# A four-layer convolution and attention sequence on one core: when v's half terms, the later weights, q's terms, the gates and one step of layer 3 are issued

## The chip, the core and the metric

The kernel runs on one core of a Trainium2 chip. The core has a matrix engine (TensorE; in the profile PE for its matmuls and PEld for its weight loads), a vector engine (VectorE, DVE), a scalar engine for activations (ScalarE, ACT), GpSimd (POOL) and SyncE (SP), which here issues nearly all DMAs. Each engine runs its own list of instructions in order, and they wait for each other through semaphores. The metric is the device time of one execution in microseconds (us); the time before is the median of three runs.

## The reference

The input x is eight images of 512 channels by 32 x 32 positions, in f32. Four layers follow one another:

```python
# layer 0: group norm, attention with 8 heads of 64, three inner steps, projection, residual
q, k, v = split(qkv_w @ group_norm(x))
h = softmax(q k^T / 8) v
for _ in range(3): h = h + 0.1 * tanh(inl_w @ h + inl_b)
x = x + proj_w @ h + proj_b
# layer 1: attention over positions, with q and k of 64 channels
x = x + softmax(q1 k1^T) v1
# layer 2: filter up by 2 in both directions, leaky relu, filter down by 2
x = down(leaky(up(x)))
# layer 3: gates from the pooled image mix 8 experts into one set of weights per image
rw = sigmoid(mean(x) @ router_w.T + router_b)
W_i = sum_e rw[e] * w_i[e]
x = relu(bn(W_3 * relu(bn(W_2 * relu(bn(W_1 * x))))) + x)      # 1x1, 3x3, 1x1
```

The gates of an image need layer 2's result of that image only. Layer 3 needs the mixed weights.

## The kernel before

Images are taken one after the other, numbered 0 to 7. For each, `layer0`, `layer1` and, between it and the next image, `between` are called. Layer 3 comes after all of them, for all images; layer 2's result of each image is written to memory (`spilled`, in the profile spill_u) and read back as z.

**Products by half terms.** Every 512 x 512 product with a weight matrix is done by Winograd's form of Strassen's scheme: seven products of quarters instead of eight. The seven are called P1, C11, U2, U3, C22, C21 and C12. Three sums are built up in PSUM (banks A: P1, C11; X: U2, U3, C21; Y: C22, C12); between its terms a bank is read by DVE or ACT. The quarter sums of the data are made on DVE (`quarter_sum`, L515; the sums 0 and 1 serve C22 and U2, the sums 2 and 3 serve U3 and C21), those of the weights lie ready in memory (`stored`) and are loaded as one tile of 1,792 KB by `weight` (L464). `in_turn` (L584) yields after each *half term* (one of the seven for one half u of the output): 14 half terms a product, each four matmuls of 256 columns in v, or two of 512 in q and k. Each matmul stands in the trace as two records. Two orders of the seven exist, `plain` and `alternate` (L593, L594); with `late` the first half of q goes by the plain one and its banks alternate between two PSUM pools.

**The stretch between two images** (`between`, L1346) is written by hand for PE, DVE, ACT and SP: what is called first stands first in each engine's list. It holds layer 1's weighted sum of image b, layer 2 of image b, and q, k and v of image b + 1. Layer 2 of an image goes by two halves e of the channels: `wide` (filter up along the rows, on PE; copies; stores to across_u), `turn` (read back turned), nine `fine_passes` (L1330: `up`, leaky relu, `down`, stores to back_u), `turn_back` (L1282: two reads of 1,024 KB each that need all stores of the half), `narrow` (L1289: two sets of matmuls, the first on the first read), `channels` (L1314: transposes zT, a copy on ACT that sums for the gates, and a spill). `fill` is called twice after each fine pass and issues one half term of k or, when k's 14 are done, of v. So the last v terms are left for the narrow passes:

```python
            for e in range(2):
                two.narrow(e, 0)
                two.narrow(e, 1)
                for _ in range(2):
                    next(value_parts)
                two.channels(e, 0)
                two.channels(e, 1)
                for _ in range(2):
                    next(value_parts)
            all_of(value_parts)
```

The weights rotate through three buffers. The loads of inl (for the inner steps), proj and v1 are issued by SP after q, before v, and at the end.

**Attention of layer 0** (`layer0`, L808) is by hand for PE, DVE and ACT: 64 steps. Step i issues `scores(i)` (four matmuls, exp on ACT, a running sum accs on DVE), then `weighted(i - 2)` (av, four matmuls). The scores' banks come from a pool of two pairs (`ps_sc`), the exps' tiles from the pool `tmp` of six, which other wide temporaries share; half-wide ones have a pool of four. After attention come the three inner steps inl_0 to inl_2, where a planner orders the engines.

**Gates.** `Router` makes them: `sums` (four products and two adds on DVE), `logits` (a matmul with ones into a pair of `ps_sc`, then one DVE operation an image), `gates` (exp on ACT, two DVE operations), `operator` (two DVE operations an image), which makes the matrix that mixes the experts. That for images 0 to 6 stands in image 7's `layer0` after the first two terms of the inner step; that for image 7 in layer 3. `blend_early` and `blend_last` then mix with matmuls (mix, mix_last) into memory.

**The end.** `last_across` (L1405) does layer 1's weighted sum and the wide passes of image 7, `last_rows` its fine passes, `last_columns` its narrow ones, with `lean_images` (L1668) as filling: a chain of steps of layer 3's images 0 and 1 (`first` is the first 1x1 product by halves, in the profile c at L1620; `second` is c2, the 3x3 product, at L1562, and c3 at L1656). The reading of z of image 1 is issued at the end of `last_across`. Images 2 to 7 then run in a loop, in which each round advances the mixing for image 7 by three steps.

Of the kernel before, what the change touches and what calls it, by code (L numbers as in the profile page):

```python
# [17 lines left out]
P = 128  # L18
B, C, H, W = 8, 512, 32, 32
S = H * W  # L20
# [37 lines left out]
def tile_sequence(ctx: ExitStack, tc: tile.TileContext, a: dict, out: bass.AP, shifted: bool):  # L58
# [181 lines left out]
    class Router:  # L240
# [4 lines left out]

        def sums(self):
            n = self.n
            t = tmp(f"parts_{self.name}", S)[:, 0 : n * CC * NE]
            parts = t.rearrange("p (b c e) -> p b c e", b=n, c=CC)
            means = pooled[:, :, self.images].rearrange("p c b -> p b c")  # L250
            for c in range(CC):
                nc.vector.tensor_tensor(
                    parts[:, :, c, :], means[:, :, c].unsqueeze(2).to_broadcast([P, n, NE]),
                    router_w[:, c, :].unsqueeze(1).to_broadcast([P, n, NE]), ALU.mult,
                )
            nc.vector.tensor_add(parts[:, :, 0:2, :], parts[:, :, 0:2, :], parts[:, :, 2:4, :])
            self.parts = parts[:, :, 0, :]
            nc.vector.tensor_add(self.parts, self.parts, parts[:, :, 1, :])
# [14 lines left out]
            nc.vector.reciprocal(at, at)  # L273

        def operator(self, to):
            here = ident.rearrange("p (g e) -> p g e", e=NE)
            for b in range(self.n):
                t = tmp(f"here_{self.name}_{b}", S)[:, 0:P].rearrange("p (g e) -> p g e", e=NE)
                gate = rw[:, self.images, :][:, b, :].unsqueeze(1).to_broadcast([P, NR, NE])
                nc.vector.tensor_tensor(t, here, gate, ALU.mult)  # L280
                nc.vector.tensor_reduce(to[:, b, :], t, AX.X, ALU.add)

    PIECES = WE // HALF
    BLOCK = CC * S // HALF
# [296 lines left out]
        elif u == 0:  # L581
            keep[what] = pair_tmp(f"{name}_{what}")

    def in_turn(name, wt, src, sums_of, made, rows=False, late=False):  # L584

        opened = 0

        terms = {
            "P1": ("A11", src[:, 0:2, 0:HALF]), "C11": ("A12", src[:, 2:4, 0:HALF]),
            "U2": ("S2", 1), "U3": ("S3", 2), "C22": ("S1", 0), "C21": ("-A22", 3),  # L590
            "C12": ("S4", src[:, 2:4, HALF:S]),
        }
        alternate = ("P1", "U2", "C11", "U3", "C22", "C21", "C12")  # L593
        plain = ("P1", "C11", "U2", "U3", "C22", "C21", "C12")  # L594
        opens = {"P1": "A", "U2": "X", "C22": "Y"}
        runs = {"P1": "A", "C11": "A", "U2": "X", "U3": "X", "C21": "X", "C22": "Y", "C12": "Y"}
        for u in range(2):
            banks = {}
            for what in plain if late and u == 0 else alternate:
                part, data = terms[what]  # L600
                part = wt[:, PARTS.index(part)]
                if isinstance(data, int):
                    data = sums_of[data]
                else:
                    data = [data[:, cc] for cc in range(2)]
                if what in opens:
                    pool = (ps_mm, ps_tp)[opened % 2] if late else ps_mm
                    opened += 1
                    banks[opens[what]] = bank(pool, f"{name}_{opens[what]}{u}")
                ps = banks[runs[what]]  # L610
                for s in range(2 if rows else 1):
                    for cc in range(2):
                        if rows:
                            at = (2 * u + s) * P
                            dst, lhs, rhs = ps[:, ts(s, QR)], data[cc][:, at : at + P], part[:, cc]
                        else:
                            dst, lhs, rhs = ps, part[:, cc, ts(u, P)], data[cc]
                        nc.tensor.matmul(  # L618
                            dst, lhs, rhs, start=(what in opens and s == 0 and cc == 0),
                            stop=(cc == 1 and s == rows), skip_group_check=True,  # L620
                        )
                made(what, u, ps)
                yield
# [137 lines left out]
    def queries(b, h, t, w):  # L761
        q = big_tile(f"q_{b}", [P, CC, S])
        made = channels(f"q_{b}", q, qkv_b[:, 0:CC], apart=b > 0)
        if b:
            return q, in_turn(f"q_{b}", w["q"], h, t, made, late=True)
        return q, product(f"q_{b}", w["q"], h, t, made)

    def keys(b, h, t, w):
# [13 lines left out]
    def first_qkv(h, w):  # L782
        made = []
        for mv in channel_stats(0, h):
            pass
        all_of(norm_factors(0, mv, made))
        group_norm(h, *made, nc.vector)
        first_sums(*held["q"], h[:, CC - 1, 0:1])
        t = quarter_sums("h_0", h)
        w["q"] = first_rest(*held["q"])  # L790
        for key in "kv":
            w[key] = weight_sums(key, *held[key], t[3][1][:, 0:1])
        q, parts = queries(0, h, t, w)
        all_of(parts)
        nc.vector.tensor_add(row_bias, row_bias, bias2)
        w["inl"] = weight("inl", 0)
        k, parts = keys(0, h, t, w)
        for _ in range(2):
            next(parts)
        early_exp(0)  # L800
        all_of(parts)
        w["proj"] = weight("proj", 0)
        v, parts = values(0, h, t, w)
        all_of(parts)
        w["v1"] = weight("v1", 0)
        return q, k, v

    def layer0(b, q, k, v, w):  # L808
        hf = big_tile(f"hf_{b}", [P, CC, S])
# [159 lines left out]
        totals = {}  # L969
        engines = mybir.EngineType  # L970
        with tc.manual_schedule(engines={engines.PE, engines.DVE, engines.Activation}):
            for i in range(steps + lag):
                if i < steps:
                    scores(i)
                if i >= lag:
                    weighted(i - lag)
                done = i - lag - SC - 1
                for g in range(1, 2 * PAIRS, 2):
                    closing_pair(g, done - g * SC)
                for g in range(2 * PAIRS, last_g):  # L980
                    closing(g, done - g * SC)
            t_hf = sum_tiles(f"hf_{b}_0")
            name = f"inl_{b}_0"

            def last_total():
                quarter_sum(t_hf, hf, 0, (0, 1))
                for at in range(3):
                    closing(last_g, at)
                quarter_sum(t_hf, hf, 1, (0, 1))
                quarter_sum(t_hf, hf, 0, (2, 3))  # L990
                quarter_sum(t_hf, hf, 1, (2, 3))

            inner = product(
                name, w["inl"], hf, t_hf, inner_step(name, hf), within=last_total
            )
            for _ in range(2):
                next(inner)
            copied(last_g)
# [3 lines left out]
        next(operators, None)  # L1002
        mixing = iter(())
        if b + 1 == B:
            router = Router(0, EARLY)
            router.sums()
            router.logits()
            router.gates()
            router.operator(blend["early"])
            mixing = blend_early()  # L1010
            next(mixing)
        all_of(inner)
# [333 lines left out]
    def between(b, eT, v, inv, y, x, mv, w):  # L1346
# [3 lines left out]
        with tc.manual_schedule(engines=hand):  # L1350
# [19 lines left out]
            q, parts = queries(b + 1, x, t, w)  # L1370
            next(parts)
            two.wide(1, 1, y, (act, act))
            next(parts)
            two.wide(1, 0, y, (act, act))
            two.turn(1)
            for cc in range(2):
                quarter_sum(t, x, cc, (2, 3))
            all_of(parts)
            w["inl"] = weight("inl", b + 1)
            k, parts = keys(b + 1, x, t, w)  # L1380
            v, value_parts = None, None

            def fill():
                nonlocal v, value_parts
                if next(parts, parts) is parts:
                    if v is None:
                        w["proj"] = weight("proj", b + 1)
                        v, value_parts = values(b + 1, x, t, w)
                    next(value_parts)

# [1 line left out]
            for e in range(2):  # L1392
# [3 lines left out]
                    next(value_parts)  # L1396
                two.channels(e, 0)
                two.channels(e, 1)
                for _ in range(2):
                    next(value_parts)  # L1400
            all_of(value_parts)
            w["v1"] = weight("v1", b + 1)
        return q, k, v

    def last_across(b, eT, v, inv, y):  # L1405
        two = Layer2(b)
        act, dve = nc.scalar.copy, nc.vector.tensor_copy
        with tc.manual_schedule(engines=hand):
# [3 lines left out]
            for what, u in weighted_rows(b, eT, v, inv, y):  # L1412
                if (what, u) == ("U3", 1):
                    two.wide(0, 0, y, (act, act))
                elif (what, u) == ("C22", 0):
                    two.wide(0, 1, y, (act, act))
                    two.turn(0)
            two.wide(1, 1, y, (act, dve))
            two.wide(1, 0, y, (act, dve))
            two.turn(1)  # L1420
            zs[1] = load_z(1)
# [255 lines left out]
        zs[b] = load_z(b)  # L1677
        wts[b] = load_weights(b)

    two = last_across(B - 1, *last)  # L1680
    chain = lean_images()
    mixing = blend_last()
    last_rows(two, chain, lambda n: load_image(2) if n == 10 else None)

# [8 lines left out]
    with tc.manual_schedule(engines={engines.PE, engines.DVE, engines.Activation}):  # L1693
# [2 lines left out]
        router = Router(B - 1, 1)  # L1696
        router.sums()
        c1(LEAN + 1, 0)
        router.logits()
        router.gates()  # L1700
        router.operator(blend["last"])
        for b in range(LEAN, B):
            more = b + 1 < B
            if b + 2 < B:
# [5 lines left out]
            h2 = tmp(f"h2_{b}", S)  # L1710
            c2(b, main, 1, True, False)
            nc.scalar.copy(one, main)
            for _ in range(2):
                next(mixing, None)
            c2(b, odd, 3, True, True)
            c2(b, main, 2, False, False)
            nc.scalar.copy(two, main)
# [92 lines left out]
```

## Time and profile before

| | |
|---|---|
| median of three runs | 3608.99 us (3602.99 to 3612.22) |
| the profiled execution's own time | 3608.0 us |
| its span, first to last instruction | 3606.2 us |
| PE busy | 3537.5 us (98%) |
| DVE, ACT busy | 2321.4 us (64%), 1318.1 us (37%) |
| mean granted TensorE clock | 0.994 |
| DMA, mean over the span | 100 GB/s |

A line of the waits tells the waiting engine, what it waited to do and at which line of the kernel, then for whom; then the sum, how often, and the longest. A line of the timeline tells start and duration, the engine, line and operation, what it writes and reads, its shape and count; in brackets the engine's idle time before it and who ended it. Busy time of overlapping matmuls is counted once.

### The profile page before, as it was taken

How to read it: one execution, taken by the hardware profiler on the slowest of the kernel's cores; microseconds unless marked ns; L12 is line 12 of the kernel's file. 1: busy time of each engine (PE TensorE's matmuls, PEld its weight loads, DVE VectorE, ACT ScalarE, POOL GpSimd, SP SyncE). 2: the span in 40 equal slices, each digit the busy share in tenths (PEclk: the TensorE clock that was granted, in tenths of full speed). 3: DMA queues.
4: the chain of work that ended last, by engine and by line, in shares of the span. 5: the costliest groups of instructions: out<-in, count | busy, mean ns of one | idle time of the engine just before them, and what ended most of it. 6: DMA issues, size and time to landing. Idle time of an engine off the chain costs nothing.

```text
span 3606.2 us, 47891 instructions
## 1 busy us (share of the span) xinstructions
PE 3537.5 (98%) x19445; PEld 1758.9 (49%) x19445; DVE 2321.4 (64%) x3130; ACT 1318.1 (37%) x1740; POOL 102.1 (3%) x140
## 2 busy tenths in 40 slices
PE   8999999999999999999999999999999999999998
PEld 4336543474435643465434743356434744347333
DVE  4787558755676557774677657775577656755544
ACT  0632345223442236323452235422362234432443
POOL 4100000000000000000000000000000000010000
PEclk9999999999999999999999999999999999999999
DMA  5102441115211350024411251023411152232783
GB/s 202 39 30 85 128 144 42 44 58 188 74 36 64 114 178 16 27 85 142 136 36 64 78 182 45 30 85 120 152 42 44 53 182 84 100 109 73 250 322 117
DMA packets 149032, 360.86 MB, mean 100 GB/s; under 512 B 17792, under 2 KB 92560, under 8 KB 142144
## 3 DMA queue, kind: packets, MB, share of 16 engines
q1 hardware_dynamic: 144336, 338.56, 28.1%
q0 software_dynamic: 4320, 18.87, 1.5%
q8 instruction: 155, 2.54, 0.3%
q14 instruction: 77, 0.63, 0.1%
q10 hardware_dynamic: 144, 0.26, 0.0%
HBM read 226.55 MB, written 118.49 MB: 96 GB/s over the span
## 4 chain that ended last, share of the span: by engine, by line
PE 93%; DMA 4%; DVE 2%; ACT 1%; SPq 0%; issue 0%; DVEq 0%; ACTq 0%
PE scores L838 12%; PE av L883 12%; PE inl_X L559 7%; PE av_X L1192 5%; PE inl_Y L559 5%; PE inl_A L559 4%; PE av_A L1192 3%; PE av_Y L1192 3%; PE v_X L559 3%; PE c L1562 2%; PE proj_X L559 2%; PE k_X L618 2%; PE up L1251 2%; PE v_Y L559 2%; PE dn L1269 2%; PE v_A L559 2%
## 5 line engine op out<-in xcount | busy, mean ns | idle before, releaser
L857 ACT ACTIVATE e<-scores 128x1024 f32<-128x1024 f32 x504 | 516.4, 1025 | 420.0 <-PE scores L838 369.2
L838 PE MATMUL scores<-q,k 64*64 64x512 f32 x4096 | 530.7, 591 | 0.0
L883 PE MATMUL av<-e,v 64*64 64x512 f32 x4096 | 528.7, 589 | 0.0
L867 DVE TENSOR_TENSOR accs<-accs,e 128x1024 f32<-128x1024 f32 x240 | 294.2, 1226 | 50.9 <-ACT e L857 47.2
L883 PEld LDWEIGHTS av<-e,v 64*64 64x64 f32 x4096 | 156.6, 133 | 282.8 <-issue 274.6
L838 PEld LDWEIGHTS scores<-q,k 64*64 64x64 f32 x4096 | 152.8, 133 | 289.9 <-issue 256.2
L559 PE MATMUL inl_X<-T_hf,w_inl 128*128 128x512 f32 x576 | 262.0, 593 | 0.4 <-DVE inl_U L714 0.3
L1258 DVE TENSOR_TENSOR fine<-up,fine 128x1024 f32<-128x1024 f32 x128 | 150.7, 1219 | 112.0 <-ACT fine L1257 108.8
L1257 ACT ACTIVATE fine<-up 128x1024 f32<-128x1024 f32 x128 | 124.0, 1020 | 159.8 <-PE up L1251 159.8
L559 PE MATMUL inl_A<-hf,w_inl 128*128 128x512 f32 x384 | 176.2, 601 | 3.7 <-DVE hf L700 3.7
L559 PEld LDWEIGHTS inl_X<-T_hf,w_inl 128*128 128x128 f32 x576 | 108.5, 190 | 138.8 <-issue 111.0
L703 ACT ACTIVATE inl_U<-inl_U,inl_b 128x512 f32<-128x512 f32 x96 | 67.0, 719 | 291.1 <-DVE inl_U L718 291.1
L904 DVE RECIPROCAL inv<-av 128x256 f32<-128x256 f32 x80 | 138.9, 1745 | 0.0
L714 DVE TENSOR_TENSOR inl_U<-inl_X,inl_P 128x512 f32<-128x512 f32 x96 | 61.8, 685 | 109.2 <-PE inl_X L559 109.2
L865 DVE TENSOR_TENSOR accs<-e,e 128x1024 f32<-128x1024 f32 x48 | 59.7, 1244 | 100.1 <-ACT e L857 81.1
L1192 PE MATMUL av_A<-v,eT 128*128 128x256 f32 x512 | 122.6, 383 | 0.0
L559 PEld LDWEIGHTS inl_A<-hf,w_inl 128*128 128x128 f32 x384 | 71.9, 191 | 101.4 <-issue 85.7
L1192 PE MATMUL av_X<-v,eT 128*128 128x256 f32 x512 | 114.0, 381 | 0.0
L1229 ACT COPY wide<-wide 128x1024 f32<-128x1024 f32 x62 | 59.8, 1015 | 135.6 <-PE wide L1221 135.6
L1081 ACT ACTIVATE eT<-scores 128x512 f32<-128x512 f32 x128 | 66.1, 603 | 115.5 <-PE scores L386 115.5
L1192 PEld LDWEIGHTS av_X<-v,eT 128*128 128x128 f32 x512 | 96.6, 190 | 19.3 <-DVE av_U L1166 6.5
L867 DVE TENSOR_TENSOR acc<-acc,e 128x1024 f32<-128x1024 f32 x80 | 96.8, 1210 | 8.4 <-ACT e L857 7.6
(398 smaller groups left out, 5551.5 us busy)
## 6 DMA issues: line engine op xcount, KB each, us to landing
x<-in_x_dram SPq DMA_DIRECT2D x64, 512.0 KB, 6.0
across_u<-wide SPq DMA_DIRECT2D x128, 256.0 KB, 3.7
turned<-across_u SPq DMA_DIRECT2D x64, 512.0 KB, 5.9
back_u<-sent SPq DMA_DIRECT2D x256, 128.0 KB, 2.3
back<-back_u SPq DMA_DIRECT2D x32, 1024.0 KB, 7.1
w_v<-stored_u_v SPq DMA_DIRECT2D x14, 1792.0 KB, 7.3
out_dram<-z SPq DMA_DIRECT2D x31, 512.0 KB, 3.0
spill_u<-z SPq DMA_DIRECT2D x28, 512.0 KB, 5.8
```

The lines of the kernel that those rows point to most:

```text
L559: nc.tensor.matmul(dst, lhs, rhs, start=(opens and s == 0 and cc == 0), stop=(cc == 1 and s == rows), skip_group_check=True,)
L618: nc.tensor.matmul(dst, lhs, rhs, start=(what in opens and s == 0 and cc == 0), stop=(cc == 1 and s == rows), skip_group_check=True,)
L838: nc.tensor.matmul(ps[r][rows[c]], k[rows[r], oc, jc * P + c * HD : jc * P + c * HD + HD], q[rows[r], oc, ts(sh, HALF)], start=True, stop= ...
L857: nc.scalar.activation(e, pair, AF.Exp, scale=HD ** -0.5)
L867: nc.vector.tensor_add(accs[g], accs[g], e)
L883: nc.tensor.matmul(avs[g][r][rows[c]], v[rows[r], jc, ts(2 * oc + c, HD)], e[rows[r], ts(c, HALF)], start=(jc == 0), stop=(jc == SC - 1),)
L904: nc.vector.reciprocal(copies[g][:, at], totals[g][:, at])
L1192: nc.tensor.matmul(ps[:, ts(s, QR)], left[:, j, at : at + P], right[:, j, :], start=(what in ("P1", "U2", "C22") and s == 0 and j == 0), s ...
L1251: nc.tensor.matmul(pairs[g // 2][HD * s : HD * s + HD, ts(g % 2, HALF)], up_v[part, :], self.turned[e][part, first : first + 2, :], start= ...
L1257: nc.scalar.mul(t, ps, 0.2)
L1258: nc.vector.tensor_max(t, ps, t)
L1269: nc.tensor.matmul(banks[s][W * g : W * g + W, :], dn_v[part, :], fine[g // 2][part, ts(g % 2, HALF)], start=True, stop=True,)
```

## The change

Five things are issued at another place; no arithmetic changes.

1. In `between`, after the first pair of `channels` four half terms of v are issued instead of two, so that none is left after the last pair of terms.
2. In `between`, the loads of inl and proj are issued at the end, ahead of that of v1.
3. q's first half goes in the order `alternate`, as its second half, k and v do; the quarter sums 2 and 3 are called one place earlier. `late` is called `two_pools` now and only chooses the pools.
4. The gates of images 0 to 6 are made in image 7's attention: from step 3 on, each step issues a piece of `early_router`: the sums at step 3, logits and gates at step 4, then one image's operator a step. Their temporaries come from the half-wide pool.
5. `last_across` takes the first step of `lean_images` between its last two wide passes (the weights' transform and half of image 0's first product), so the chain runs one step ahead of where it was; and in layer 3's loop the gates of image 7 are made inside the first round, in the place of its first two mixing steps.

```diff
+        def operators(self, to):
             here = ident.rearrange("p (g e) -> p g e", e=NE)
             for b in range(self.n):
-                t = tmp(f"here_{self.name}_{b}", S)[:, 0:P].rearrange("p (g e) -> p g e", e=NE)
+                t = tmp(f"here_{self.name}_{b}")[:, 0:P].rearrange("p (g e) -> p g e", e=NE)
...
                 nc.vector.tensor_reduce(to[:, b, :], t, AX.X, ALU.add)
+                yield
...
-            for what in plain if late and u == 0 else alternate:
+            for what in alternate:
...
+    def early_router():
+        router = Router(0, EARLY)
+        router.sums()
+        yield
+        router.logits()
+        router.gates()
+        yield
+        yield from router.operators(blend["early"])
...
+            router = iter(early_router() if b + 1 == B else ())
             for i in range(steps + lag):
                 if i < steps:
                     scores(i)
+                if i > 2:
+                    next(router, None)
                 if i >= lag:
                     weighted(i - lag)
...
         if b + 1 == B:
-            router = Router(0, EARLY)
-            router.sums()
-            router.logits()
-            router.gates()
-            router.operator(blend["early"])
             mixing = blend_early()
...
             next(parts)
             two.wide(1, 1, y, (act, act))
+            for cc in range(2):
+                quarter_sum(t, x, cc, (2, 3))
             next(parts)
             two.wide(1, 0, y, (act, act))
             two.turn(1)
-            for cc in range(2):
-                quarter_sum(t, x, cc, (2, 3))
             all_of(parts)
-            w["inl"] = weight("inl", b + 1)
...
                     if v is None:
-                        w["proj"] = weight("proj", b + 1)
                         v, value_parts = values(b + 1, x, t, w)
...
-                for _ in range(2):
+                for _ in range(4 - 2 * e):
                     next(value_parts)
             all_of(value_parts)
-            w["v1"] = weight("v1", b + 1)
+            for key in ("inl", "proj", "v1"):
+                w[key] = weight(key, b + 1)
...
             two.wide(1, 1, y, (act, dve))
+            next(chain)
             two.wide(1, 0, y, (act, dve))
...
-    two = last_across(B - 1, *last)
     chain = lean_images()
+    two = last_across(B - 1, chain, *last)
...
         c1(LEAN + 1, 0)
-        router.logits()
-        router.gates()
-        router.operator(blend["last"])
         for b in range(LEAN, B):
...
             nc.scalar.copy(one, main)
-            for _ in range(2):
-                next(mixing, None)
+            if b > LEAN:
+                for _ in range(2):
+                    next(mixing, None)
+            else:
+                router.logits()
+                router.gates()
+                router.operator(blend["last"])
             c2(b, odd, 3, True, True)
```

More of the change, by code (lines that the diff above doesn't have):

```diff
@@ L247, in sums @@
             n = self.n
-            t = tmp(f"parts_{self.name}", S)[:, 0 : n * CC * NE]
+            t = tmp(f"parts_{self.name}")[:, 0 : n * CC * NE]
             parts = t.rearrange("p (b c e) -> p b c e", b=n, c=CC)
@@ L275, in operator @@
         def operator(self, to):
+            for _ in self.operators(to):
+                pass
+        def operators(self, to):
             here = ident.rearrange("p (g e) -> p g e", e=NE)
             for b in range(self.n):
-                t = tmp(f"here_{self.name}_{b}", S)[:, 0:P].rearrange("p (g e) -> p g e", e=NE)
+                t = tmp(f"here_{self.name}_{b}")[:, 0:P].rearrange("p (g e) -> p g e", e=NE)
                 gate = rw[:, self.images, :][:, b, :].unsqueeze(1).to_broadcast([P, NR, NE])
@@ L582, in hold, with in_turn @@
             keep[what] = pair_tmp(f"{name}_{what}")
-    def in_turn(name, wt, src, sums_of, made, rows=False, late=False):
+    def in_turn(name, wt, src, sums_of, made, rows=False, two_pools=False):
         opened = 0
@@ L593, in in_turn @@
         alternate = ("P1", "U2", "C11", "U3", "C22", "C21", "C12")
-        plain = ("P1", "C11", "U2", "U3", "C22", "C21", "C12")
         opens = {"P1": "A", "U2": "X", "C22": "Y"}
@@ L606, in in_turn @@
                 if what in opens:
-                    pool = (ps_mm, ps_tp)[opened % 2] if late else ps_mm
+                    pool = (ps_mm, ps_tp)[opened % 2] if two_pools else ps_mm
                     opened += 1
@@ L764, in queries @@
         if b:
-            return q, in_turn(f"q_{b}", w["q"], h, t, made, late=True)
+            return q, in_turn(f"q_{b}", w["q"], h, t, made, two_pools=True)
         return q, product(f"q_{b}", w["q"], h, t, made)
@@ L1398, in between, with last_across @@
                 two.channels(e, 1)
-                for _ in range(2):
+                for _ in range(4 - 2 * e):
                     next(value_parts)
             all_of(value_parts)
-            w["v1"] = weight("v1", b + 1)
+            for key in ("inl", "proj", "v1"):
+                w[key] = weight(key, b + 1)
         return q, k, v
-    def last_across(b, eT, v, inv, y):
+    def last_across(b, chain, eT, v, inv, y):
         two = Layer2(b)
```

## The prediction

> **What bounds the kernel now.** I read the page first, then the waits of TensorE (PE), then the timeline of the stretches that they name. Busy shares say that PE sets the end:
>
> ```profile
> span 3606.2 us, 47891 instructions
> PE 3537.5 (98%) x19445; PEld 1758.9 (49%) x19445; DVE 2321.4 (64%) x3130; ACT 1318.1 (37%) x1740; POOL 102.1 (3%) x140
> ```
>
> PE's waits (us in total, times, longest) show what the other 2% are:
>
> ```profile
> PE narrow L1304 <- DMA back<-back_u: 24.3, 14, 3.3
> ...
> PE q_X L618 <- DVE q_U L639: 6.0, 7, 0.9
> ...
> PE inl_A L559 <- DVE hf L700: 3.7, 1, 3.7
> ```
>
> No matmul is removed, so only waits can go, and what hangs on them. Largest is layer 2's second narrow pass, once in each of seven images. Image 0, PE by time; the first pass (478.03) is the yardstick for the second (489.51):
>
> ```profile
> 476.21 1.89 PE L618 MATMUL v_X<-w_v,T_h 128*128 128x256 f32 x8
> 478.03 1.95 PE L1304 MATMUL narrow<-back,dn_h 64*32 64x512 f32 x32
> ...
> 486.94 1.89 PE L618 MATMUL v_A<-w_v,x 128*128 128x256 f32 x8
> 489.51 1.09 PE L1304 MATMUL narrow<-back,dn_h 64*32 64x512 f32 x16 [0.69 <-DMA back<-back_u]
> 493.11 1.96 PE L1304 MATMUL narrow<-back,dn_h 64*32 64x512 f32 x16 [2.50 <-DMA back<-back_u]
> 495.00 3.78 PE L618 MATMUL v_X<-w_v,T_h 128*128 128x256 f32 x8
> ```
>
> The wait is 3.2 us, and then the same v term takes 3.78 us instead of 1.89. The windows' clock column shows why (us, PE busy ... PEclk, DMA share, GB/s):
>
> ```profile
> 476.20:483.40 7.20, 7.20 (x57) 4.92 (x56) 4.50 (x6) 0.00 (x0) 0.00 (x0) 1.00 0.80 300
> 486.90:500.40 13.50, 10.31 (x57) 6.24 (x57) 5.18 (x7) 0.00 (x0) 0.00 (x0) 0.75 0.58 202
> ```
>
> The issues of SP's queue, same place, show why the data is late:
>
> ```profile
> 474.43 0.37 SPq L468 DMA_DIRECT2D w_proj<-stored_u_proj  x1
> 475.33 1.94 SPq L1278 DMA_DIRECT2D back_u<-sent  x4
> 483.82 1.01 SPq L1287 DMA_DIRECT2D back<-back_u  x2
> ```
>
> The last four stores to back_u stand behind a weight load of 1,792 KB; the read-back, which needs them landed, goes out 6.55 us after the last was issued (475.33 + 1.94 to 483.82), where the median back_u store lands in 2.3 us.
>
> [...]
>
> **The change part by part.**
>
> *v's terms spread, weights loaded later (between).* Two v terms move from after the second pair of channel passes to before the second narrow pass: 2 x 1.72 us of PE (spacing of v_A and v_X starts, 486.94 - 485.21) slide into the wait. Waits per image are 3.2, 4.1, 3.8, 2.7, 3.3, 4.0, 3.2; 3.44 covers all but 0.7, 0.4 and 0.6. The proj and inl loads go behind the last spill, so the last stores should land at about 477.3 + 2.3 and the read-back start about 4 us sooner. Either cover nearly suffices; together some 4 us are spare. With no wait the clock stays up. Price: from the term before the pass to the first transpose, the first pass takes 7.26 us (476.21 to 483.46) in every image; the second takes 13.49, 13.85, 13.03, 10.29, 12.49, 13.24, 12.40, sum 88.8, against 7 x 7.26 = 50.8. Gain **38.0**; I keep 0.5 for remains.
>
> What may be late next? C11 follows P1 after one term of 1.72, and P1's two DVE adds take 1.29: free. Before attention two terms (3.44) instead of four follow the last transposes; ACT needs 1.2 us after them to free the scores' bank: free. The fifth exp writes where a z tile is being spilled: the spill goes out about 0.4 us after the last transpose and lands in 5.8 (median), while that exp comes 3.44 + 7 x 0.86 = 9.5 later: 3 us spare, weights queued behind it. inl, proj and v1 are needed when attention is over, over 100 us later; nothing on SP's queue is due before the sums' copies. Cost 0.
>
> *q in k's order.* U3 no longer stands next to U2 in one bank. The 0.85 us wait is U2's add on DVE (0.69), seven times: gain **6.0**. DVE's order does not change: the sums 2 and 3 ran already at 402.58 to 405.07, before U2's matmuls would end (405.6). C11's activation goes behind two more ACT copies; its bank is wanted some 15 us later. If that cover fails, 0.9 an image.
>
> *Router beside scores (image 7).* Before, its DVE operations stood among the inner step's. From inl_A's start to inl_X's: 15.40 us (3119.04 to 3134.44), in image 6 8.18 (2703.31 to 2711.49); minus 1.72 of matmul pulled forward and 0.2 for the router's own: gain **5.3** (3.69 of wait, the rest half clock). The cost: the router's matmul now stands in PE's order right behind scores 4 and needs sums that DVE does after accs 3. These lines are the place (DVE, then PE):
>
> ```profile
> 3008.94 2.55 DVE L867 TENSOR_TENSOR accs<-accs,e 128x1024 f32<-128x1024 f32 x2
> ...
> 3009.57 1.04 PE L838 MATMUL scores<-q,k 64*64 64x512 f32 x8
> 3010.43 1.04 PE L883 MATMUL av<-e,v 64*64 64x512 f32 x8
> ```
>
> accs 3 ends at 3011.49. Six router operations as in the old place (0.13 apart, then 0.28 and 0.22) take 1.2, and from the last sum to its matmul 0.14 (3451.66 to 3451.80): 3012.84, where PE could start at 3010.43. Cost **2.4**; queued behind are av 2 and all later scores. A wait of that length brought half clock at most narrow passes, though not in image 3; [...] The later pairs (2 x 0.20 us a step) fit DVE's 0.29 to 0.49 idle. Bounds 0 (sums early) to 4.5.
>
> *Layer 3 step between the last wide passes.* The step is 1.72 us of matmul, one ACT and three DVE operations on weights issued at 3291.7 to 3294.6. It takes the place of the 1.14 us wait there; the wide pass ends at 3351.95 as before, the first up waits about 1.5 instead of 1.1, since a DVE copy now stands behind the three. But the whole chain comes a step earlier, and the first half of z_1's product now stands before up 2 and down 1:
>
> ```profile
> 3359.77 2.01 SPq L1239 DMA_DIRECT2D turned<-across_u  x4
> 3361.82 2.12 SPq L1455 DMA_DIRECT2D z<-spill_u  x4
> ...
> 3366.55 1.11 PE L1251 MATMUL up<-turned,up_v 32*64 32x512 f32 x16
> 3367.60 1.09 PE L1269 MATMUL dn<-fine,dn_v 64*32 64x512 f32 x16
> 3369.64 4.84 PE L1620 MATMUL c<-z,weights 128*128 128x512 f32 x8 [0.95 <-DMA z<-spill_u]
> ```
>
> z_1 leaves SP behind the turn at 3361.82 and its first piece lands at 3369.6; nothing moves that. PE gets there at 3351.95 + 1.5 + 1.05 (up) + 3.44 + 2.1 (up, down) + 1.72 = 3361.8: a wait near 7.8. Then 1.72 + 2.1 + 1.72 end at 3375.2, before 3374.4: loss 0.8. After so long a wait 3.4 to 6.8 us at half clock cost 1.7 to 3.4, taken 2.5. Later, `two`'s copy is covered (0.68, twice), the last router's 0.97 wait too, as c2 stands ahead of it; the c3 waits of 1.41, 2.61 and 1.13 become about 1.5, 2.2 and 1.2. Gain 2.6, net **-0.7**; bounds -5 to +4. The last mixing moves to image 5; its weights are wanted some 29 us later, and store (5.2) plus load (5.6) fit.
>
> Sum: 38.0 - 0.5 + 6.0 + 5.3 - 2.4 - 0.9 - 0.7 = 44.8. The profiled execution took 3608.0 (span 3606.2 and 1.8 around it), so 3563.2; the median shown is 1.0 above it: **3564**.
>
> **Rivals.** (1) *The narrow waits go, a smaller one comes* at the same place: transposes on DVE's copies, or C11 on P1's adds, 2 us an image. DVE's 64% and the 0.3 us of slack at C11 speak for it, the first pass without a wait against. 44.8 - 14 = 31: 3578. (2) *The last stage is better*: z_1's load lands sooner, or the clock holds, and the early sums don't stall: 7 more, 3557. For it: DMA is idler; against: SP's fixed order. (3) *Slower*: at the start of attention the weight burst (5.4 MB) overtakes the z spills, and the fifth exp waits for its tile. It decides from 44.8/7 = 6.4 us of new wait an image, so a spill of 0.4 + 5.8 + 3 + 6.4, near 16 us; 10 us of it make 25 more: 3634. For it: proj's load held the back_u stores so; against: there the stores stood behind the load, here they stand ahead. (4) *No change*: the clock and the waits return elsewhere in full, since PE was late for data that stays late: 3609. Against: the data's lateness comes from a load that is gone.
>
> **How the numbers follow.** Likeliest 0.72, its own range 3559 to 3571; (1) 0.12, (2) 0.09, (3) 0.04, (4) 0.03. 3556 to 3580 holds the first three and leaves the rest and the tails out. Faster, same and slower count from 0.3%, about what a measurement here can tell (10.8 us): 0.93, 0.03, 0.04.
>
> **What would show it.** PE's waits for back gone or under 2 us in sum, seven stretches of about 7.3 us and clock 1.00 there; the back read issued some 2.5 us after the last store; q_X's wait gone; in image 7 none at inl_A, but a router wait near 2.4 in attention; a wait for z near 8 in the last stage. The prediction is wrong if scores or exp wait at attention's start, or if narrow still waits over 1 us an image.

## The result: 3565.03 us, and the profile after

| | before | after |
|---|---|---|
| median of four runs each (us) | 3609.97 (3602.99 to 3612.22) | 3565.03 (3562.41 to 3567.08) |
| the profiled execution's own time | 3608.0 | 3565.32 |
| its span | 3606.2 | 3563.5 |
| mean granted TensorE clock | 0.994 | 0.997 |

The ratio is 0.9878, with a 95% interval of 0.9861 to 0.9895: faster, by four times the 0.3% that can be told from no change. The forecast was 3564. That the two lie so near is in part luck: the sum holds errors of both signs that nearly cancel, the largest of them in the last stage. (The kernel before has one run more here than in the table ahead of the prediction.)

The page of the changed kernel, engines: as many matmuls as before, PE at 99% of a shorter span.

```profile
span 3563.5 us, 47886 instructions
PE 3520.5 (99%) x19445; PEld 1753.9 (49%) x19445; DVE 2321.2 (65%) x3130; ACT 1318.2 (37%) x1740; POOL 102.3 (3%) x140
```

PE's waits in the changed kernel (us in total, times, longest). The waits for back, of q_X and of inl_A, which led this list before, are not in it. What leads it now (apart from the start's 11.0, which both kernels have) is new or larger: z, c twice, and the router.

```profile
PE c L1631 <- DMA z<-spill_u: 7.2, 1, 7.2
PE c L1667 <- DVE z L1670: 4.9, 2, 3.8
PE c L1631 <- DVE z L1670: 2.6, 1, 2.6
PE router L263 <- DVE parts L258: 2.1, 1, 2.1
```

**The narrow passes.** PE's timeline in image 0, changed kernel. The second narrow pass, with two v terms after it, runs as one group of 32 without a gap, and no term takes over 2.0 us:

```profile
488.40 1.89 PE L622 MATMUL v_A<-w_v,x 128*128 128x256 f32 x8
490.22 1.95 PE L1315 MATMUL narrow<-back,dn_h 64*32 64x512 f32 x32
...
495.66 1.91 PE L1333 MATMUL zT<-ident,narrow 128*128 128x128 f32 x16
```

From the term ahead of the pass to the first transpose it is 488.40 to 495.66, 7.26 us; the windows' row for just that stretch (PE busy first, the clock third from the end) has PE busy throughout at full clock (1.00), and no DMA:

```profile
488.40:495.66 7.26, 7.26 (x58) 4.92 (x58) 4.50 (x6) 0.00 (x0) 0.00 (x0) 1.00 0.00 0
```

SP's issues at the same place: the eight stores to back_u go out without a weight load among them, and the read-back follows 1.99 us after the last was issued (469.77 + 5.27 to 477.03), where it was 6.55. The loads of inl and proj follow at 499.24, behind the spills:

```profile
469.77 5.27 SPq L1289 DMA_DIRECT2D back_u<-sent  x8
477.03 1.00 SPq L1298 DMA_DIRECT2D back<-back_u  x2
```

**The last stage.** PE's timeline at the end of image 7's layer 2, changed kernel. The product of z_1 stands ahead of its data and waits 7.17 us; c3 waits 3.82, and the product behind it 2.61. Two of the groups that follow a wait take about twice their time (3.75 for four records of c at 3319.69, 3.55 at 3361.10, where 1.98 is usual); the granted clock there is 0.5, from 3316.50 for 6.83 us and from 3360.87 for 3.41 us:

```profile
3319.69 3.75 PE L1631 MATMUL c<-z,weights 128*128 128x512 f32 x4 [7.17 <-DMA z<-spill_u]
...
3352.53 1.98 PE L1667 MATMUL c<-h,weights 128*128 128x512 f32 x4 [3.82 <-DVE z L1670]
...
3361.10 3.55 PE L1631 MATMUL c<-z,weights 128*128 128x512 f32 x4 [2.61 <-DVE z L1670]
```

Dated by the first matmul of each product on PE, the two profiled executions compare so, stage by stage (us; a plus is time gained):

| stage | forecast | measured |
|---|---|---|
| start of k to start of attention, seven images | 38.0 - 0.5 | 38.0 (6.23, 6.59, 5.77, 3.04, 5.23, 5.98, 5.15) |
| q, seven images | 6.0 | 7.9 (28.98 to 27.85 in each) |
| attention of image 7 | -2.4 - 0.9 | -2.7 (114.67 to 117.33) |
| inner steps of image 7 | 5.3 | 5.9 (91.28 to 85.43) |
| from image 7's projection to the end | -0.7 | -6.7 (388.21 to 394.95) |
| before all this, to k of image 0 | 0 | 0.9 |
| sum | 44.8 | 43.2 |

The 0.9 at the start is no part of the change: the first 16 records of q_A took 9.23 us in this execution and 10.06 in that of before. Between their last matmuls the two differ by 43.2, in span by 42.7.

### The profile page after: what moved, and what is told of

Read it like the earlier page. It is cut to its first block, busy times and chain, and to the rows that moved or that the text cites. A ratio compares the mean times of both kernels' runs of the same rounds, so it can differ in the third digit from the quotient of the medians.

```text
span 3563.5 us, 47886 instructions
## 1 busy us (share of the span) xinstructions
PE 3520.5 (99%) x19445; PEld 1753.9 (49%) x19445; DVE 2321.2 (65%) x3130; ACT 1318.2 (37%) x1740; POOL 102.3 (3%) x140
## 4 chain that ended last, share of the span: by engine, by line
PE 97%; DVE 1%; DMA 1%; ACT 0%; issue 0%; POOL 0%; DVEq 0%; ACTq 0%; POOLq 0%; SPq 0%
PE scores L851 12%; PE av L896 12%; PE inl_X L564 7%; PE av_X L1203 5%; PE inl_Y L564 5%; PE inl_A L564 5%; PE av_A L1203 3%; PE av_Y L1203 3%; PE v_X L564 3%; PE proj_X L564 2%; PE k_X L622 2%; PE c L1573 2%; PE q_X L622 2%; PE v_X L622 2%; PE up L1262 2%; PE v_Y L564 2%
```

## The experiments

All are edits of the changed kernel. Each was timed in four executions or more, beside the kernel before at 3607.3 to 3607.4; each profile is of one execution. The changed kernel's 3565.03 was measured earlier, beside 3609.97, so that a difference of 2 or 3 us between its median and one below says little by itself; there the stretches in the profiles decide.

**Which of the two covers removes the narrow waits?** First both undone, then each alone.

*Both undone.* The v terms go 2, 2, 2, 2 again, and inl and proj are loaded in their old places; the other parts of the change stay.

```diff
+            w["inl"] = weight("inl", b + 1)
             k, parts = keys(b + 1, x, t, w)
...
+                        w["proj"] = weight("proj", b + 1)
...
-                for _ in range(4 - 2 * e):
+                for _ in range(2):
                     next(value_parts)
...
-            for key in ("inl", "proj", "v1"):
-                w[key] = weight(key, b + 1)
+            w["v1"] = weight("v1", b + 1)
```

> Both are undone, the rest of the change stays. Theory: the seven second narrow passes take 38 us more than the changed kernel's, 24 of it waits and the rest half clock; span 3563.5 + 38 = 3601.5. Rival (part of the gain of 38 came from elsewhere): under 3595.

Measured: 3601.63 us (3596.69 to 3607.49), ratio to before 0.9988 [0.9981, 0.9995]. The waits of that kernel:

```profile
PE narrow L1315 <- DMA back<-back_u: 21.9, 13, 3.3
```

The seven stretches from k to attention are 33.0 us longer than with both covers (5.04, 5.46, 5.11, 2.91, 6.35, 4.46, 3.63): 21.9 of it is wait; behind the waits of 0.81 and 2.48 in image 0, the v term takes 2.56 us instead of 1.89. So the pair carries 33 of the 38 in these two profiles; by the medians it is worth 36.6. The other 5 are 2.4 of wait (24.3 before) and about as much that the list of waits does not hold: in image 0 the v term behind the wait took 3.78 us in the kernel before, where the granted clock was 0.50 for 6.83 us, and 2.56 here. Why this kernel's waits are a little shorter was not settled.

*The v terms alone* (the loads at their old places, as in the first two and the last hunk above).

> The loads of inl and proj go back to their old places; v's terms stay as changed. Theory (either cover nearly suffices): the read-back is late as before, about 3.2, 4.1, 3.8, 2.7, 3.3, 4.0, 3.2 us past the old start of the narrow pass, and 3.44 us of v terms cover all but 0.7, 0.4 and 0.6: waits for back of about 1.7 us in sum, no half clock at the narrow passes, span about 3565 against 3563.5. Rival (the load is the cause, and only its removal helps): the stretch from the term before the second narrow pass to the transposes stays near 10 us and above, and the span comes out above 3580.

Measured: 3568.56 us (3564.49 to 3569.15), ratio 0.9891 [0.9874, 0.9907].

```profile
PE narrow L1315 <- DMA back<-back_u: 3.5, 4, 2.2
```

The waits are twice the 1.7 us expected; behind the longest, 2.23 us in image 0, the v term takes 1.99 us, as in the changed kernel. The stretches are 4.7 us longer in sum than in the changed kernel, 2.46 of it in image 0 and 1.05 in image 1. There proj's load still stands among the stores (SP issues it at 471.95 and four stores behind it at 472.83), and the read-back goes out at 481.65, 6.59 us after the last of them was issued; in the changed kernel it goes out at 477.03, 1.99 us after, and the stores land 1.9 to 2.3 us after their issue. Image 0 waits although the two terms should have covered it: from the read-back's issue to the second set of matmuls it is 11.38 us (481.65 to 493.03), where it was 9.29 in the kernel before (483.82 to 493.11).

*The late loads alone* (the terms 2, 2, 2, 2, as in the middle hunk).

> v's terms go back to 2, 2, 2, 2 and the rest at the end; the loads stay late. Theory: the read-back is issued about 2.5 us after the last store instead of 6.6, lands by about 9.3 us after that, which is just when the pass without the two terms begins: waits for back under 3 us in sum, clock 1.00, span about 3564. Rival (the terms are what matters, the store and read chain is late by itself): waits for back of 12 us and more in sum, half clock at several passes, span above 3580.

Measured: 3565.64 us (3562.34 to 3566.52), ratio 0.9887 [0.987, 0.9903], the changed kernel's time. Its list of PE waits has none for back, down to 0.7 us, and every stretch is within 0.05 us of the changed kernel's. Its PE timeline in image 0 shows how early the pass comes without the two terms ahead of it, and that the data is there:

```profile
486.64 1.95 PE L1315 MATMUL narrow<-back,dn_h 64*32 64x512 f32 x32
```

From the read-back's issue to the pass it is 9.75 us here (476.89 to 486.64) and 13.19 in the changed kernel: the terms' spread adds 3.44 us of reserve to a wait that the loads have already removed, and no time. The second read, the later one, lands 3.9 to 5.8 us ahead of its matmuls in the changed kernel; less the 3.44 that leaves 0.5 to 2.4 here, an estimate.

**q's order.** The first half goes by the plain order again, nothing else:

```diff
-            for what in alternate:
+            for what in plain if two_pools and u == 0 else alternate:
```

> Only q's first half goes back to the plain order of its terms (C11 ahead of U2, so that U3 follows U2 in the same bank); everything else as in the changed kernel. Theory (the order is worth what its stretch shows): the waits of q_X for q_U return, about 0.85 us in each of seven images (6.0 in sum, 7 times), and the stretch of q's fourteen terms grows from 27.85 to 28.98 us; the time is 6.0 to 7.9 us above the changed kernel. Rival: the waits in front of U3 were gone because the sums of layer 2 stand elsewhere; then there is no wait and under 1 us of difference.

Measured: 3574.55 us (3574.22 to 3574.97), ratio 0.9907 [0.9891, 0.9924], 9.5 above the changed kernel. The waits of this run:

```profile
PE q_X L623 <- DVE q_U L644: 6.0, 7, 0.9
```

Each q stretch takes 28.97 or 28.98 us instead of 27.85, 7.9 in all, so the order is the cause. The profile has another 1.69 in image 7's attention, which q's order does not touch; where it comes from was not shown. The prediction took 0.85 an image, the wait alone, and the stretch lost 1.12. The timeline of this run shows the other 0.27 at the term behind the wait:

```profile
408.43 1.98 PE L623 MATMUL q_X<-T_h,w_q 128*128 128x512 f32 x4 [0.85 <-DVE q_U L644]
```

Terms without a wait in this stretch start 1.72 apart though each lasts 1.88: they overlap by 0.16. A wait takes that overlap away, and the term behind it lasts 1.98 instead of 1.88: 0.85 + 0.16 + 0.10 = 1.11. The trace models where a matmul ends, so this split is its own; the 1.12 rests on starts alone.

**The gates of images 0 to 6.** *Back behind attention:*

```diff
-            router = iter(early_router() if b + 1 == B else ())
+            router = iter(())
...
         if b + 1 == B:
+            for _ in early_router():
+                pass
             mixing = blend_early()
```

> Only the first router goes back behind the attention of image 7, where it stood before. Theory (two terms, 5.85 gained at inl against 2.66 lost in attention): the wait of inl_A for hf returns at about 3.7 us with a half-clock stretch behind it, attention of image 7 gets 2.7 us shorter, its wait for the router's sums is gone, and the time is 3.2 us above the changed kernel. The prediction's own sizes give 2.0. Rival: the inl wait was shortened by something else, for instance v's terms or the late loads; then removing the router from attention leaves the kernel 2.7 us faster.

Measured: 3567.19 us (3565.68 to 3570.46), ratio 0.9885 [0.9868, 0.9901], 2.2 above the changed kernel, too little to go by. In its profile attention of image 7 is 114.67 us again, 2.66 shorter, and the inner steps 91.60, 6.17 longer: 3.5 net, with the old wait at its old place, and 3.50 us for the four records behind it, where 1.98 is usual:

```profile
3085.71 3.50 PE L564 MATMUL inl_A<-hf,w_inl 128*128 128x512 f32 x4 [3.70 <-DVE hf L704]
```

So the gain at inl is the router's removal from there, and not a gift of the other parts.

*The router's matmul two score steps later*, its sums where they are:

```diff
         router.sums()
         yield
+        yield
+        yield
         router.logits()
```

> The router's matmul goes two score steps further back, its sums stay where they are. Theory (the 2.1 us wait is only that its sums need DVE behind accs 3): the wait is gone, attention of image 7 goes from 117.3 to about 114.9 us, and inl has none still; the time is 2.1 to 2.7 us below the changed kernel. Rival: DVE is so full in this stage that the pairs of the operator, now two steps later, delay the accs and bring the wait back at the scores or at inl; then the time stays within 1 us of the changed kernel.

Measured: 3563.35 us (3562.94 to 3567.21), ratio 0.9879 [0.9862, 0.9895], 1.7 below the changed kernel, which these few executions can't tell from none. Its profile can: image 7's attention takes 115.33 us, 2.00 less, and nothing is lost behind it. The router in PE's timeline of this run has no wait in brackets, where the changed kernel has 2.10:

```profile
2967.61 0.43 PE L263 MATMUL router<-parts,ones 128*128 128x56 f32 x2
```

Of the 2.66 lost in attention 0.66 stays: the matmul itself (0.43), which merely moved, and its joints. The wait is an order of issue, as the prediction had it, and DVE has room for the pairs.

**The last stage.** *No step between the last wide passes*: `next(chain)` is left out of `last_across`, and the chain runs as before the change.

> The layer 3 step between the last wide passes is taken out, so the chain runs as in the kernel before. Theory (running one step ahead costs more than it brings): the wait for z falls from 7.2 to under 2 us, the waits among c3 from 9 to about 5, half clock in the last stage once instead of three times; from image 7's projection to the end 5 to 8 us less, span about 3557. Rival (the last stage lost its time to the gates' other place or to the mixing): no gain here, span 3562 to 3566.

Measured: 3560.09 us (3558.47 to 3563.1), ratio 0.9873 [0.9856, 0.9889], 4.9 below the changed kernel; from the projection to the end its profile has 6.8 us less. So the edit of `last_across` costs about what the table of stages says, and the new place of the last gates costs nothing that shows.

*The step kept, the next filling held back*, so that from the second fine pass on the chain stands where it stood before:

```diff
-            next(chain, None)
+            if done != 1:
+                next(chain, None)
             done += 1
```

> The layer 3 step between the last wide passes stays, but the filling after the next fine pass issues none, so that from there on the chain of the first images stands where it stood before the change. Theory (what is lost in the last stage is the chain's being a step ahead, not the step's place): no wait of 7 us for z; c waits for DVE are 1.4, 2.6 and 1.1 as before; the half clock comes once or not at all in the last stage; its length is 6 to 8 us below that of the changed kernel, so the time is near 3558 to 3560. Rival (the step's place costs: DVE's three operations there delay the first up): the last stage stays within 2 us of the changed kernel's.

Measured: 3562.26 us (3560.54 to 3563.04), ratio 0.9873 [0.9857, 0.989]. The stretch from the projection to the end is 6.4 us shorter than the changed kernel's, within the 6 to 8 expected; the median is only 2.8 lower, where 5 to 7 were expected. The profiled execution itself took 3560.54, 4.8 less than the changed kernel's, with a start that is 1.6 later; the others have no profile, and what their 2.8 lacks is left open. The waits of c for DVE in this run:

```profile
PE c L1668 <- DVE z L1671: 5.2, 3, 2.6
```

The wait for z is 4.5 us; the c waits are those of the kernel before (5.2 in 3), with the step still in its new place. So it is the chain's standing one step ahead that made the first 3.8 instead of 1.4; the step's place does not cost. How the clock stood in this run was not shown; the changed kernel's is at 0.50 in three stretches of the stage (6.83 us from 3316.50, 3.41 from 3360.87, 3.41 from 3391.59), and how much of the 6.4 is theirs is left open. A wait of 4.5 for z is left, against 1.0 before the change, for the most part because PE gets to z_1 2.5 us sooner after the projection's start: in the kernel before the granted clock was 0.50 ahead of it, for 6.83 us from 3352.35.

*z_1's loads ahead of the second turn* on SP's queue, all else as in the changed kernel:

```diff
-            two.turn(1)
             zs[1] = load_z(1)
+            two.turn(1)
```

> Only the loads of z_1 go ahead of the second turn on SP's queue, where they need not wait for the stores of the wide passes to land: they leave right behind the last of those stores, some 5.3 us sooner (about 3306.7 instead of 3311.98). Theory (the wait of 7.2 us is that queue's order): the wait for z falls to about 2, and with it the half clock behind it; the first of the three losses of the last stage is gone, the c waits for DVE stay at 3.8, 2.6 and 1.1: 5 to 8 us below the changed kernel, near 3558. Rival (the turn's reads are then late by the same 2 us or more, and up waits for them, or the loads land no sooner since the stores hold the DMA engines): less than 2 us below.

Measured: 3557.64 us (3556.6 to 3559.13), ratio 0.9869 [0.9852, 0.9885], 7.4 below the changed kernel. SP's queue of the changed kernel, then of this run. There z waits behind turned, and turned for the stores to land (their issues end at 3306.72); here z goes out right behind them (3307.56):

```profile
3309.93 2.02 SPq L1250 DMA_DIRECT2D turned<-across_u  x4
3311.98 2.03 SPq L1466 DMA_DIRECT2D z<-spill_u  x4
```

```profile
3307.66 2.57 SPq L1466 DMA_DIRECT2D z<-spill_u  x4
3311.27 4.59 SPq L1250 DMA_DIRECT2D turned<-across_u  x4
```

PE in this run: the wait of 7.17 is 0.36 for ACT and 0.65 for z, and the four records of c behind it (3318.27) take the usual 1.98 us; c3's 3.82 is as it was, and the half clock now follows there (3.78 for what takes 1.98):

```profile
3315.15 1.12 PE L1631 MATMUL c<-z,weights 128*128 128x512 f32 x2 [0.65 <-DMA z<-spill_u]
...
3345.36 3.78 PE L1667 MATMUL c<-h,weights 128*128 128x512 f32 x4 [3.82 <-DVE z L1670]
```

The stage is 8.8 us shorter, more than the wait. Half clock went with it: behind the wait for z the changed kernel's clock was 0.50 for 6.83 us, and the c there took 3.75 for four records. From 3336.00 to 3352.00 this run's clock is 0.79 on average. The turn's reads took 4.59 us to issue instead of 2.02, and no up waits for them.

**Together.** The step held, z_1's loads first, the router's matmul later:

> Three edits together: the filling after the next fine pass issues no step, z_1's loads go ahead of the second turn, and the router's matmul goes two score steps back. If they add up: 3.3 (the step held) + 4.5 to 6.2 (the wait of 4.5 that was left there, and its half clock) + 2.0 (the router's wait) below the changed kernel's 3565.0, so 3553.5 to 3555. If the z loads only move the wait to the turn's reads: near 3560.

Measured: 3553.04 us (3550.7 to 3553.42), ratio to before 0.9855 [0.9839, 0.9871]. It adds up: 12.0 below the changed kernel, where 10.0 to 11.5 were expected. From the projection to layer 3's last gates the profile lists four groups of PE waits for this run, 8.2 us in all, none of them for z or the router; the first two are the largest. The granted clock of the stretch is 1.00.

```profile
PE c L1670 <- DVE z L1673: 5.2, 3, 2.6
PE c L1576 <- ACT two L1654: 1.4, 2, 0.7
```

Its slowest execution is 9.0 us below the changed kernel's fastest; the two were each timed beside the kernel before, not beside each other.

*The same without the step* (`next(chain)` left out, z_1 first, the router later):

> No step between the last wide passes, z_1's loads ahead of the second turn, the router's matmul two score steps back. Adding up from the kernel without the step (3560.1): 2.3 for its two waits for z, 2.0 for the router, so near 3555.8; the two waits of 1.1 us for ACT at the last wide pass and the first up stay, and with them the half clock of 3.4 us or more that followed them. If instead the step, once z comes in time, is worth its covering one of these two waits, this kernel is 1 to 3 us behind the one that keeps it and holds the next.

Measured: 3553.13 us (3552.46 to 3553.63), ratio 0.9855 [0.9839, 0.9872]: 2.7 better than expected, and no different from the kernel with the step held. Once z comes in time, the step between the wide passes is worth nothing that a time shows. The two waits of 1.1 us that it was to cover are there. Without the other two edits what followed them was slow: the up took 2.33 us (1.66 at its place in the changed kernel) and eight records of c 5.57, where 3.70 is usual; how this run's clock stood there was not shown. The stage is 4.3 us shorter than without those edits, 2.3 of it the waits for z, and 1.3 longer than with the step held.

## Why the prediction was right, point by point

**The narrow passes: right in size and cause.** 38.0 was taken from the first pass as the yardstick, and 38.0 came. The 0.5 kept for remains was not needed. "Either cover nearly suffices; together some 4 us are spare" was right of the loads, which suffice alone, and of the spare time, which is 3.9 to 5.8 us; the terms alone leave 4.7 us.

**What was costed at nothing there: right.** Attention of images 1 to 6 has its 114.67 us to 0.01, so neither the exp's tile nor the scores' banks came late; the spills go out ahead of the weights on SP, and the slower rival has no ground.

**q: right cause, size 1.9 short.** The term "0.85 us wait, seven times" was the wait alone; the whole loss was 1.12, with the overlap and the slower term behind it.

**The router: right in kind.** The wait was 2.1 where 2.4 was worked out; inl gained 5.9 for 5.3. The 0.9 for half clock was the author's estimate: half of 3.41 us, the length of five of the eight stretches at 0.50 in the profile before, at half a chance. It did not come in the changed kernel, whose clock is 1.00 from 2962.60 to 2972.00; with v's terms alone the av behind the same wait took 1.99 us instead of 1.09.

**The last stage: the step that failed.** The wait for z was forecast near 7.8 and was 7.17, with half clock behind it as forecast (0.50 for 6.83 us): to the end of the first z_1 product the loss is 2.8, where -0.8 - 2.5 = -3.3 was taken. What failed is "the c3 waits of 1.41, 2.61 and 1.13 become about 1.5, 2.2 and 1.2", and with it the gain of 2.6. The covers in that gain came: both waits of 0.68 for `two`'s copy and the last router's 0.97 are gone. But the c3 waits, which were to stay about as they were, became 3.82, 2.61 and 1.13, with 0.33 and 0.54 of new ones for ACT, and two more stretches of half clock of 3.41 us each (from 3360.87 and from 3391.59). The timelines of DVE and of ACT in the changed kernel show the shape of the largest:

```profile
3345.94 1.40 DVE L1670 SCALAR_TENSOR_TENSOR z<-c,g,z 128x512 f32<-128x512 f32 x2
3349.46 2.36 DVE L1269 TENSOR_TENSOR fine<-up,fine 128x1024 f32<-128x1024 f32 x2 [2.12 <-ACT fine L1268]
```

```profile
3347.37 1.15 ACT L1673 ACTIVATE z<-z,b 128x1024 f32<-128x1024 f32 x1 [3.58 <-DVE z L1670]
3348.43 1.92 ACT L1268 ACTIVATE fine<-up 128x1024 f32<-128x1024 f32 x2
```

The first pair of z comes late, since the three operations of the weights' transform (0.55 + 0.56 + 0.56) stand ahead of it on DVE. ACT has the activation of z ahead of the next fine pass's two operations, so it sits idle for 3.58 us until that pair is done; DVE then waits 2.12 for ACT's fine, and its second pair of z (3351.74), which frees the bank for PE's c3 at 3352.53, stands behind. Before the change a fine pass stood between c2 and the first c3, so ACT's fine was issued ahead of any activation of z, and the wait was 1.41. The prediction took the waits for c as a sum that moves with the chain, without writing out DVE's and ACT's orders at the new places; that the chain's position makes the longest of them is shown by the run with the next filling held, the handing-over itself is read from the timeline.

**The sum.** 0.5 + 1.9 + 1.2 better in three places, 6.0 worse in one, and 0.9 at the start that no one forecast: 44.8 became 43.2 on PE and 42.7 in the profiled span. That these nearly cancel is luck. The rivals: no smaller wait took the narrow waits' place; the last stage was not better, though with two edits it becomes so (382.5 us, 5.7 less than before the change).

## What to carry to other kernels

When stores whose landing is awaited share a queue with a load that nothing needs soon, move the load first: here that alone removed every wait for back, where rearranging the waiting engine's work instead left 4.7 us. When a chain of filling is moved ahead by one step, write out at its new places what each of the other engines has in order before it, and do it for every step of the chain, not only for the one that moves. And price a removed wait by the stretch against its undisturbed twin: the idle time in brackets leaves out the lost overlap (1.12 us lost for 0.85 of wait) and the half clock behind it (a v term of 3.78 us instead of 1.89).

## What the runs showed of the hardware that was not expected

The wait of q_X cost more than its idle time although the clock held (1.00 from 400.85 to 430.00 in the kernel before): 1.12 us for 0.85, in each of seven images and again when the order was put back.

Ahead of the last matmul the profile before has eight stretches at a granted clock of 0.50, three of 6.83 us and five of 3.41, the changed kernel's three, one of 6.83 and two of 3.41. The same wait brings one in one execution and none in another. c3's wait of 3.82 us is in the changed kernel and in the run with z_1's loads first. The windows' rows around it (length, PE busy ... the clock third from the end), changed kernel, then the other, where the clock goes to half within the wait:

```profile
3347.22:3350.64 3.42, 1.50 (x4) 0.38 (x2) 1.30 (x3) 3.27 (x4) 0.00 (x0) 1.00 0.45 109
3350.64:3354.05 3.41, 1.52 (x4) 0.68 (x4) 2.85 (x5) 1.55 (x3) 0.00 (x0) 1.00 0.91 292
```

```profile
3340.72:3344.14 3.42, 0.83 (x2) 0.00 (x0) 1.84 (x2) 3.42 (x5) 0.00 (x0) 1.00 0.37 97
3344.14:3347.55 3.41, 2.19 (x3) 1.15 (x4) 1.90 (x4) 1.15 (x1) 0.00 (x0) 0.50 1.03 348
```

The changed kernel's wait of 2.61 brought 0.50 for 3.41 us from 3360.87; the same wait in the kernel before did not, whose clock is 1.00 from 3399.00 to 3408.00. The router's 2.10 is a third case, above. What decides between them was not shown. So half clock behind these waits of 2.1 to 3.8 us could not be told from the wait's length, and part of the changed kernel's loss in the last stage is chance.

The read-back behind a weight load of 1,792 KB was issued 6.55 us after the last store, and 1.99 us after it when the load was not there: the loads' place on the queue alone made 4.6 us, as the run with only the loads moved back shows (6.59).
